# Scores for the softmax maxima spread over four row groups, in banks of three key tiles, interleaved with the scores of the weights

## The chip, the cores and the metric

The kernel runs on one core of a Trainium2 chip. The metric is device time in microseconds (us). The kernel before takes 2109.02 us, the median of three runs (2106.92 to 2109.55). One further execution was profiled; everything said of engines, waits and durations comes from its trace. TensorE (PE in the profile) multiplies matrices into PSUM, which has 8 banks of 128 x 512 float32; VectorE is DVE, ScalarE is ACT, GpSimd is POOL, SyncE is SP.

## The reference

Four blocks with residuals on x of shape (2, 1024, 512), all float32: a gated linear recurrence, a feed-forward block with ternary weights, differential attention, and the same feed-forward block again. The change touches the attention alone:

```
q = concat(heads(x @ Wq1), heads(x @ Wq2))       # 32 query heads, d = 32
k2, v2 = repeat(k, 2), repeat(v, 2)              # 16 heads of keys and values
scores = einsum('bhqd,bhkd->bhqk', q, k2) * scale
scores = where(causal, scores, finfo.min)
p = softmax(scores)
y = einsum('bhqk,bhkd->bhqd', p, v2)             # T = 1024 queries and keys
y = y1 - sigmoid(x @ Wlam) * y2
out = y @ Wo
```

A softmax needs the maximum of each query's row before the exponential. Queries and keys come in eight tiles of 128 each, so a head has 36 tiles of scores at or under the diagonal.

## The kernel before

The attention works on `pairs` of heads (L821): 32 pairs, in each of which the two heads are e = 0 and 1. Everything of a pair is made twice.

**Maxima.** The scores are first computed with queries on the partitions (`maxima_step`, L933; matmul L947, called s in the profile), and DVE reduces them along the keys to one negated maximum per query: `tensor_reduce` (L962) for blocks off the diagonal, and a masked form (L957) for blocks that end on it. Nothing but the maxima is kept. `split_maxima` (L967) writes each maximum as three bfloat16 parts on POOL, and `turn_maxima` (L983) transposes them on TensorE, so that they lie along the queries.

**Weights.** Then the scores are computed again with keys on the partitions (`weights_step`, L995; matmul L1008, called t), three rows of ones times the turned maxima are added in the same bank (L1016), ACT takes the exponential out of the bank (L1024), POOL zeroes what lies over the diagonal (L1027), and `weigh` (L1034; matmul L1046, called y) multiplies the weights with the values and accumulates in a bank of its own. A unit is one tile of 128 keys against one block of 512 queries or what of it the diagonal leaves (512, 384, 256 or 128 columns); there are 12 units, and a step takes two of them.

**Row groups.** A head has 32 dimensions, so a matmul of scores fills 32 of TensorE's 128 rows. Queries and keys are kept twice, in swapped halves, so that `operands(pair, i, e)` (L897) finds head e in row group 2i + e. Unit 0 of a step uses row groups 0 and 1, unit 1 uses 2 and 3. Each such float32 matmul becomes two weight loads and two matrix instructions in the profile.

**Order.** From the second part of the attention on, TensorE's instructions stand in the order of the source (`manual_schedule`, L1226); the loop is at L1228 to L1237. The other engines' order is made by a scheduler. A step of pair n is: the scores t of its two units (four banks), their subtractions, the maxima of three banks of pair n + 1, the products y of the step before, and then work `beside` it (projections, turned maxima, layer norms and so on). There are six steps to a pair, 31 pairs with a following one, and the maxima of pair 0 are made ahead of the loop between the products of `values`. The table `max_banks` (L920) spreads 18 banks of 512 columns over the six steps, three to a step, in three row groups.

**Banks.** Seven PSUM banks form one ring (`ps_ring`, L776; `ring_bank`, L780) for everything but y. A new tile takes the bank of the seventh tile before it, and its first matmul waits until that one's last reader is done.

Of the kernel before, what the change touches and what calls it, by code (L numbers as in the profile page):

```python
# [10 lines left out]
F32 = mybir.dt.float32  # L11
# [3 lines left out]
ALU = mybir.AluOpType  # L15
AX = mybir.AxisListType

P = 128
# [5 lines left out]
BLK = 512  # L24
# [18 lines left out]
def kernel(  # L43
# [15 lines left out]
    nc = tc.nc  # L59
# [66 lines left out]
    def layernorm_end(mv, rstd):  # L126
        nc.vector.reciprocal(rstd, rstd)
        return mv, rstd
# [103 lines left out]
    with ExitStack() as s:  # L232
# [65 lines left out]
        start = wa.tile([P, BLK], F32, name="a_start")  # L298
# [103 lines left out]
        first = Input(0)  # L402
# [27 lines left out]
        for t in range(NBLK):  # L430
            yt = wa.tile([P, NKC, BLK], F32, tag="yt", name=f"yt{t}")
            last = t == NBLK - 1
            for c in range(NKC):
                n = f"{t}_{c}"
# [9 lines left out]
                u = ap_.tile([P, BLK], F32, tag="u", name=f"u{n}")  # L444
                if t + c == 0:
# [3 lines left out]
                    following = Input(1, layernorm_end(*measured.root()))  # L449
# [22 lines left out]
                a = ap_.tile([P, BLK], F32, tag="a", name=f"a{n}")  # L472
# [53 lines left out]
                elif last and c == 1:  # L526

                    room = xt_pool.tile([P, NKC, D], F32, tag="xt", name="xn_f0_0")
# [9 lines left out]
            products = [(j, k) for j in range(TPB) for k in range(NKC)]  # L538
# [3 lines left out]
            po = {}  # L542
# [22 lines left out]
            if not last:  # L565
                q, rq = q_next, rq_next
                following = Input(t + 2, stats) if t + 2 < NBLK else None
# [11 lines left out]
    NQ = SEQ // P  # L579
# [188 lines left out]
    QB = BLK // P  # L768
    HV = HD + 1
    with ExitStack() as s:  # L770


        b_a, b_p, b_b, b_c, b_d = (
            s.enter_context(tc.tile_pool(name=f"b_{i}", bufs=1, reuse_waits="tile")) for i in "apbcd"
        )
# [4 lines left out]
        def ring_bank(name, dtype=F32):  # L780
            return ps_ring.tile(
                [P, BLK if dtype == F32 else 2 * BLK], dtype, tag="ring", name=name
            )


        causal = b_c.tile([P, BLK], BF, name="causal")
# [21 lines left out]
        for i in range(4):  # L808
# [12 lines left out]
        pairs = [  # L821
            (b, g, p, par)
            for b in range(NT // SEQ) for g in range(NG) for p in range(2) for par in range(2)
        ]
        groups, nmax, lams, totals, shares, factors = {}, {}, {}, {}, {}, {}
# [71 lines left out]
        def operands(pair, i, e):  # L897

            b, g, p, par = pair
            rows = ts(2 * i + e, HD)  # L900
            return (groups[b, g, kind][rows, int(i != p), :] for kind in (2, par))

        def name(pair):
            return "_".join(map(str, pair))
# [2 lines left out]


        fills = {
            "a": [(2, 0, 384), (0, 0, 128)],  # L910
            "b": [(1, 0, 256), (5, 512, 256)],
            "c": [(3, 0, 512)],
            "d": [(4, 0, 512)],
            "e": [(5, 0, 512)],
            "f": [(6, 512, 384), (4, 512, 128)],
            "g": [(6, 0, 512)],
            "h": [(7, 0, 512)],
            "i": [(7, 512, 512)],
        }
        max_banks = [  # L920
            [(e, i, fills[f]) for f, e, i in step]
            for step in (

                [("d", 0, 1), ("d", 1, 1), ("e", 0, 0)],
                [("c", 0, 1), ("a", 1, 1), ("a", 0, 0)],
                [("g", 0, 1), ("g", 1, 1), ("e", 1, 0)],
                [("c", 1, 1), ("b", 0, 1), ("b", 1, 0)],
                [("h", 0, 1), ("f", 1, 1), ("f", 0, 0)],
                [("h", 1, 1), ("i", 0, 1), ("i", 1, 0)],
            )  # L930
        ]

        def maxima_step(pair, step):  # L933


            if step == 0:
                nmax[pair] = b_a.tile(
                    [P, 2, NQ, 2], F32, tag="nmax", name=f"nmax{name(pair)}", bufs=2
                )
            maxima_of = nmax[pair].rearrange("p f j e -> p (f j e)")  # L940
            for x, (e, i, products) in enumerate(max_banks[step]):
                po = ring_bank(f"s{name(pair)}_{step}_{x}")
                keys, queries = operands(pair, i, e)
                at_col, made = 0, []
                for j, first, nk in products:
                    part = po[:, at_col : at_col + nk]
                    nc.tensor.matmul(  # L947
                        part, queries[:, ts(j, P)], keys[:, first : first + nk],
                        start=True, stop=True,
                    )  # L950
                    made.append((part, (first // BLK * NQ + j) * 2 + e, first + nk == (j + 1) * P))
                    at_col += nk
                for part, place, diagonal in made:
                    top = maxima_of[:, place : place + 1]
                    if diagonal:

                        nc.vector.tensor_tensor_reduce(  # L957
                            part, part, causal[:, BLK - part.shape[-1] :], -1.0, 3.0e38,
                            ALU.add, ALU.min, top,
                        )  # L960
                    else:
                        nc.vector.tensor_reduce(top, part, AX.X, ALU.max, negate=True)  # L962

        turned = {}
        n_maxima = [0]
# [1 line left out]
        def split_maxima(pair, half):  # L967

            m = maxima[n_maxima[0] % 4]
            n_maxima[0] += 1  # L970
            src = nmax[pair][:, 0, ts(half, QB), :]
            if half:
                nc.vector.tensor_tensor(src, src, nmax[pair][:, 1, ts(half, QB), :], ALU.min)
            part = m.rearrange("p j (d e r) -> p j d e r", d=2, e=2)
            rest = b_a.tile([P, QB, 2], F32, tag="mrest", name=f"mrest{name(pair)}_{half}", bufs=2)
            nc.gpsimd.tensor_copy(part[:, :, 0, :, 0], src)
            nc.gpsimd.tensor_sub(rest, src, part[:, :, 0, :, 0])
            nc.gpsimd.tensor_copy(part[:, :, 0, :, 1], rest)
            nc.gpsimd.tensor_sub(part[:, :, 0, :, 2], rest, part[:, :, 0, :, 1])
            nc.gpsimd.tensor_copy(part[:, :, 1, :, 0:3], part[:, :, 0, :, 0:3])  # L980
            turned[pair, half] = m
# [10 lines left out]
        units = [(qb, kb) for qb in range(2) for kb in range((qb + 1) * QB)]  # L992
        outs = {}

        def weights_step(pair, step):  # L995

            made, banks = [], {}
            for u in (2 * step, 2 * step + 1):  # L1000
                qb, kb = units[u]
                lo = max(0, kb - qb * QB) * P
                made.append((u, kb, lo, BLK - lo, kb >= qb * QB))
            for i, (u, kb, lo, nq, _) in enumerate(made):
                for e in range(2):
                    keys, queries = operands(pair, i, e)
                    banks[u, e] = ring_bank(f"t{name(pair)}_{u}_{e}")
                    nc.tensor.matmul(  # L1008
                        banks[u, e][:, :nq], keys[:, ts(kb, P)],
                        queries[:, (qb + 1) * BLK - nq : (qb + 1) * BLK],  # L1010
                        start=True, stop=False,
                    )
            for i, (u, kb, lo, nq, _) in enumerate(made):
                for e in range(2):
                    rows = slice(64 * i + 32 * e, 64 * i + 32 * e + 3)
                    nc.tensor.matmul(  # L1016
                        banks[u, e][:, :nq], ones[rows], turned[pair, qb][rows, lo:],
                        start=False, stop=True,
                    )
            steps = []  # L1020
            for u, kb, lo, nq, diagonal in made:
                pr = b_a.tile([P, 2, BLK], F32, tag="pr", name=f"pr{name(pair)}_{u}", bufs=4)
                for e in range(2):
                    nc.scalar.activation(pr[:, e, :nq], banks[u, e][:, :nq], AF.Exp)  # L1024
                if diagonal:

                    nc.gpsimd.affine_select(  # L1027
                        out=pr[:, :, :P], in_=pr[:, :, :P], compare_op=ALU.is_ge, fill=0.0,
                        base=0, pattern=[[0, 2], [1, P]], channel_multiplier=-1,
                    )  # L1030
                steps.append((pair, u, pr))
            return steps
# [115 lines left out]
        for n, pair in enumerate(pairs):  # L1148
            b, g, p, par = pair
            following = pairs[n + 1] if n + 1 < len(pairs) else None  # L1150
# [45 lines left out]
        n = len(pairs) - 1  # L1196
# [30 lines left out]
        waiting = []  # L1227
        for n, pair in enumerate(pairs):  # L1228
            for step in range(STEPS):
                made = weights_step(pair, step)  # L1230
                if n + 1 < len(pairs):
                    maxima_step(pairs[n + 1], step)
                for w in waiting:
                    weigh(*w)
                waiting = made
                for f, args in beside.get((n, step), ()):
                    f(*args)  # L1237
# [89 lines left out]
```

## Time and profile before

| | us |
|---|---|
| median of the runs | 2109.02 |
| the profiled execution | 2108.97 |
| its span, first to last instruction | 2107.3 |
| attention's loop over pairs and steps | 794.4 to 1705.0 of the span |
| TensorE's busy time in that loop | 909.48 of 910.60 |
| DVE's | 485.21 |
| ACT's | 379.51 |
| POOL's | 180.94 |

Times in the timeline are counted from the start of the span. A row such as "1106.30 1.03 PE L947 MATMUL s<-gr,gr 32*128 32x512 f32 x6" says: from 1106.30 on, for 1.03 us, TensorE ran six instructions of line 947, with 32 rows by 128 columns of weights, on 512 moving columns. Their ends are modelled. Brackets at the end of a row give the engine's idle time before it and who ended it. PEld is the loading of weights, which overlaps with matmuls.

### The profile page before, as it was taken

The page shows a single profiled execution, that of the slowest core. Times are in us where ns is not written, and L with a number is a line of the kernel's source. Part 1 is how long each engine was busy: PE and PEld are TensorE (multiplying, and loading weights), DVE is VectorE, ACT ScalarE, POOL GpSimd, SP SyncE. Part 2 cuts the span into 40 slices and gives each one's busy share as a digit, 9 for nine tenths or more (in the row PEclk, how much of TensorE's full clock was granted, in tenths as well). Part 3 has the DMA queues.
Part 4 walks back from the last instruction along what each step waited for, and adds up shares of the span by engine and source line. Part 5 has one row for each costly group of instructions (what it writes and reads, how often), then busy time and mean ns, then how long its engine had stood idle before and what let it go on. Part 6 is the DMA issues. An engine that isn't in the chain of part 4 may idle for free.

```text
span 2107.3 us, 28066 instructions
## 1 busy us (share of the span) xinstructions
PE 2087.2 (99%) x10624; PEld 1238.5 (59%) x10632; DVE 1102.9 (52%) x2279; ACT 826.1 (39%) x1581; POOL 461.5 (22%) x812
## 2 busy tenths in 40 slices
PE   8999999999999999999999999999999999999998
PEld 4444444788888844444444444444444447888887
DVE  5877778344345344545554555454546653443432
ACT  4444343333344313444344413244434523333432
POOL 1422313122121211212221213121212231122212
PEclk9999999999999999999999999999999999999999
DMA  7121212400000011111111101201010033000000
GB/s 274 60 90 60 90 75 77 193 1 1 1 1 14 22 47 48 37 29 36 31 37 24 41 8 38 60 17 48 20 33 14 14 113 135 20 1 21 1 21 20
DMA packets 50999, 98.71 MB, mean 47 GB/s; under 512 B 10800, under 2 KB 19120, under 8 KB 50864
## 3 DMA queue, kind: packets, MB, share of 16 engines
q1 hardware_dynamic: 50864, 96.93, 14.0%
q8 instruction: 83, 1.36, 0.3%
q14 instruction: 52, 0.43, 0.1%
HBM read 58.75 MB, written 16.78 MB: 36 GB/s over the span
## 4 chain that ended last, share of the span: by engine, by line
PE 94%; DVE 4%; issue 1%; POOL 0%; ACT 0%; DMA 0%; DVEq 0%; SPq 0%; ACTq 0%; POOLq 0%
PE y L1046 13%; PE g L664 11%; PE u L664 11%; PE f_out L685 11%; PE s L947 10%; PE pq L879 8%; PE t L1008 8%; PE pv L844 3%; PE pq L328 2%; PE a_out L546 2%; PE b_out L1115 2%; PE pa L328 2%; PE pv L328 2%; PE pg L328 2%; PE pk L328 2%; PE mt L987 1%
## 5 line engine op out<-in xcount | busy, mean ns | idle before, releaser
L1024 ACT ACTIVATE pr<-t 128x512 f32<-128x512 f32 (+3 forms) x768 | 314.8, 496 | 382.1 <-PE t L1016 381.9
L957 DVE CUSTOM_DVE_ANT_0 s<-s,causal 128x128 f32<-128x128 f32 (+3 forms) x512 | 245.2, 510 | 124.9 <-PE s L947 116.2
L1046 PE MATMUL y<-pr,val 128*64 128x512 f32 (+3 forms) x1536 | 292.0, 501 | 0.4 <-ACT ys L1063 0.2
L679 POOL TENSOR_TENSOR ssq<-ssq,sq 128x512 f32<-128x512 f32 x120 | 154.7, 1289 | 589.4 <-ACT sq L678 589.4
L962 DVE TENSOR_REDUCE nmax<-s 128x1 f32<-128x512 f32 x256 | 164.9, 686 | 182.7 <-PE s L947 182.6
L664 PE MATMUL g<-xs,w 128*128 128x512 f32 x1024 | 257.7, 394 | 0.0
L685 PE MATMUL f_out<-w,hs 128*128 128x512 f32 x1024 | 254.3, 390 | 0.3 <-DVE hs L673 0.3
L670 DVE TENSOR_TENSOR h<-h,u 128x512 f32<-128x512 f32 x128 | 88.0, 688 | 317.5 <-PE u L664 305.2
L664 PE MATMUL u<-xs,w 128*128 128x512 f32 x1024 | 253.2, 389 | 0.0
L947 PE MATMUL s<-gr,gr 32*128 32x512 f32 (+3 forms) x1536 | 251.0, 493 | 0.5 <-DVE nmax L957 0.5
L664 PEld LDWEIGHTS u<-xs,w 128*128 128x128 f32 x1024 | 192.2, 188 | 40.6
L685 PEld LDWEIGHTS f_out<-w,hs 128*128 128x128 f32 x1024 | 191.5, 188 | 40.6 <-DVE hs L673 1.1
L664 PEld LDWEIGHTS g<-xs,w 128*128 128x128 f32 x1024 | 190.0, 188 | 39.6 <-issue 1.0
L1046 PEld LDWEIGHTS y<-pr,val 128*64 128x64 f32 x1536 | 93.5, 136 | 180.8 <-issue 105.5
L1008 PE MATMUL t<-gr,gr 32*128 32x512 f32 (+3 forms) x1536 | 198.8, 533 | 0.0
L879 PE MATMUL pq<-b_xt,w_qk 128*128 128x512 f32 x384 | 176.0, 603 | 0.0
L947 PEld LDWEIGHTS s<-gr,gr 32*128 32x128 f32 x1536 | 148.5, 185 | 46.4 <-issue 14.6
L1027 POOL TENSOR_SCALAR_AFFINE_SELECT pr<-pr 128x256 f32<-128x256 f32 x256 | 102.1, 412 | 332.0 <-ACT pr L1024 332.0
L672 ACT CAST hs<-h 128x512 fp32r<-128x512 f32 x128 | 79.4, 620 | 234.3 <-DVE h L670 234.3
L669 ACT ACTIVATE h<-g 128x512 f32<-128x512 f32 x128 | 76.6, 599 | 230.6 <-PE g L664 230.5
L673 DVE TENSOR_TENSOR hs<-h,hs 128x512 fp32r<-128x512 f32 x128 | 88.6, 692 | 87.2 <-ACT hs L672 87.2
L879 PEld LDWEIGHTS pq<-b_xt,w_qk 128*128 128x128 f32 x384 | 69.7, 189 | 88.0 <-issue 74.0
(164 smaller groups left out, 2234.9 us busy)
## 6 DMA issues: line engine op xcount, KB each, us to landing
w<-w_kept SPq DMA_DIRECT2D x32, 768.0 KB, 8.6
w_kept<-w SPq DMA_DIRECT2D x16, 768.0 KB, 3.2
gr<-gr SPq DMA_DIRECT2D x96, 128.0 KB, 2.3
w<-in_w_gu_dram SPq DMA_DIRECT2D x32, 256.0 KB, 2.9
share<-ys SPq DMA_DIRECT2D x128, 64.0 KB, 2.0
x<-in_x_dram SPq DMA_DIRECT2D x16, 256.0 KB, 6.1
w<-in_w_pt_dram SPq DMA_DIRECT2D x16, 256.0 KB, 3.4
w_qk<-in_wq_dram SPq DMA_DIRECT2D x8, 512.0 KB, 4.2
```

Of the source, the lines that this page charges most:

```text
L328: nc.tensor.matmul(po, w[:, k, ts(c, P)], xt[:, k, :], start=(k == 0), stop=(k == NKC - 1))
L664: nc.tensor.matmul(po, ws[f][:, part, ts(k, P)], xs[:, e, k, :], start=(k == 0 and e == 0), stop=(k == NKC - 1 and e == 1),)
L679: nc.gpsimd.tensor_add(ssq, ssq, sq)
L685: nc.tensor.matmul(po[j], hp[:, e, ts(j, P)], ws[f][:, 2, :], start=(f == 0 and e == 0), stop=(f == NF - 1 and e == 1),)
L879: nc.tensor.matmul(po, w[:, k, ts(kind, P)], xts[b][:, k, ts(e, BLK)], start=(k == 0), stop=(k == NKC - 1),)
L947: nc.tensor.matmul(part, queries[:, ts(j, P)], keys[:, first : first + nk], start=True, stop=True,)
L957: nc.vector.tensor_tensor_reduce(part, part, causal[:, BLK - part.shape[-1] :], -1.0, 3.0e38, ALU.add, ALU.min, top,)
L962: nc.vector.tensor_reduce(top, part, AX.X, ALU.max, negate=True)
L1008: nc.tensor.matmul(banks[u, e][:, :nq], keys[:, ts(kb, P)], queries[:, (qb + 1) * BLK - nq : (qb + 1) * BLK], start=True, stop=False,)
L1024: nc.scalar.activation(pr[:, e, :nq], banks[u, e][:, :nq], AF.Exp)
L1027: nc.gpsimd.affine_select(out=pr[:, :, :P], in_=pr[:, :, :P], compare_op=ALU.is_ge, fill=0.0, base=0, pattern=[[0, 2], [1, P]], channel_mu ...
L1046: nc.tensor.matmul(y[64 * e : 64 * e + 64, lo:], all_values[:, HV * (NH * kb + h) : HV * (NH * kb + h) + 64], pr[:, e, : BLK - lo], start= ...
```

## The change

The maxima's 36 key tiles a head are cut anew: twelve pieces, most of three tiles (384 columns), some of two or four. 24 banks for the two heads take the place of 18; each step has four, one in each row group (`max_banks`). The reductions become 28 a pair in place of 24, and a query tile's maximum now comes from up to three pieces, so `split_maxima` has one more minimum for its second half.

`weights_step` becomes `row_phase`, and takes over the maxima of the following pair. Two banks for maxima (x = 0 and 1, row groups 2 and 3) are taken from the ring before all else. Then follow in TensorE's order: the scores of unit 0 (row groups 0 and 1), maxima 0 and 1 (row groups 2 and 3), the subtractions of unit 0, the scores of unit 1 (2 and 3), maxima 2 (0 or 1), the subtractions of unit 1, maxima 3 (the other of 0 and 1). The ring keeps its seven banks. Lines after the change are higher by up to 25: s is L949, t L1019, the subtraction L1029, y L1071.

```diff
         fills = {
-            "a": [(2, 0, 384), (0, 0, 128)],
-            "b": [(1, 0, 256), (5, 512, 256)],
-            "c": [(3, 0, 512)],
-            "d": [(4, 0, 512)],
...
+            "j01": [(1, 0, 2, 0), (0, 0, 1, 0)],
+            "j2": [(2, 0, 3, 0)],
+            "j3": [(3, 0, 4, 0)],
+            "j4a": [(4, 0, 3, 0)],
+            "j4b": [(4, 3, 2, 1)],
+            "j5a": [(5, 0, 3, 0)],
+            "j5b": [(5, 3, 3, 1)],
+            "j6a": [(6, 0, 3, 0)],
+            "j6b": [(6, 3, 3, 1)],
+            "j67": [(7, 7, 1, 2), (6, 6, 1, 2)],
+            "j7a": [(7, 0, 4, 0)],
+            "j7b": [(7, 4, 3, 1)],
         }
+
         max_banks = [
...
+            [(0, 1, "j2"), (1, 1, "j2"), (0, 0, "j5a"), (1, 0, "j4b")],
+            [(0, 1, "j3"), (1, 1, "j3"), (0, 0, "j01"), (1, 0, "j01")],
+            [(0, 1, "j5b"), (1, 1, "j5b"), (1, 0, "j5a"), (0, 0, "j4b")],
+            [(0, 1, "j4a"), (1, 1, "j4a"), (0, 0, "j6a"), (1, 0, "j67")],
+            [(0, 1, "j6b"), (1, 1, "j6a"), (1, 0, "j6b"), (0, 0, "j67")],
+            [(0, 1, "j7a"), (1, 1, "j7a"), (0, 0, "j7b"), (1, 0, "j7b")],
         ]
 
+        def maxima_bank(pair, step, x):
+            if step == 0 and x == 0:
+                nmax[pair] = b_a.tile(
+                    [P, 2 * NQ, 2], F32, tag="nmax", name=f"nmax{name(pair)}", bufs=2
+                )
+            return ring_bank(f"s{name(pair)}_{step}_{x}")
+
+        def maxima_of(pair, step, x, po):
+            tops = nmax[pair].rearrange("p j e -> p (j e)")
+            e, i, fill = max_banks[step][x]
+            keys, queries = operands(pair, i, e)
+            at_col, made = 0, []
+            for j, first, nk, slot in fills[fill]:
+                part = po[:, at_col : at_col + nk * P]
+                nc.tensor.matmul(
+                    part, queries[:, ts(j, P)], keys[:, first * P : (first + nk) * P],
+                    start=True, stop=True,
+                )
...
             if half:
-                nc.vector.tensor_tensor(src, src, nmax[pair][:, 1, ts(half, QB), :], ALU.min)
+                nc.vector.tensor_tensor(src, src, nmax[pair][:, NQ + QB : 2 * NQ, :], ALU.min)
+                top = nmax[pair][:, NQ - 2 : NQ, :]
+                nc.vector.tensor_tensor(top, top, nmax[pair][:, NQ + 2 : NQ + QB, :], ALU.min)
...
+            room = [maxima_bank(following, step, x) for x in range(2)] if following else []
+            scores(0)
+            for x, po in enumerate(room):
+                maxima_of(following, step, x, po)
+            subtract(0)
+            scores(1)
+            if following:
+                maxima_of(following, step, 2, maxima_bank(following, step, 2))
+            subtract(1)
+            if following:
+                maxima_of(following, step, 3, maxima_bank(following, step, 3))
...
             for step in range(STEPS):
-                made = weights_step(pair, step)
-                if n + 1 < len(pairs):
-                    maxima_step(pairs[n + 1], step)
+                made = row_phase(pair, pairs[n + 1] if n + 1 < len(pairs) else None, step)
                 for w in waiting:
                     weigh(*w)
```

In `max_banks` an entry is (head e, operand copy i, piece), and x is its place in the row; in `fills` it is (query tile, first key tile, number of key tiles, slot of the result).

## The prediction

> **What bounds the kernel now.** I read the page's busy times and its chain first, then the loop's stretch alone, then the timeline of single steps, last the groups of DVE.
>
> ```profile
> PE 2087.2 (99%) x10624; PEld 1238.5 (59%) x10632; DVE 1102.9 (52%) x2279; ACT 826.1 (39%) x1581; POOL 461.5 (22%) x812
> PE 94%; DVE 4%; issue 1%; POOL 0%; ACT 0%; DMA 0%; DVEq 0%; SPq 0%; ACTq 0%; POOLq 0%
> 794.40:1705.00 910.60, 909.48 (x6115) 433.69 (x6112) 485.21 (x1404) 379.51 (x885) 180.94 (x575) 1.00 0.12 31
> ```
>
> TensorE sets the end, and in the attention's loop it rests for 1.1 of 910.6 us. So a step's time is the time of TensorE's instructions in it, and whatever holds TensorE is paid in full. Two steps and a half of pair 10:
>
> ```profile
> 1101.60 0.70 PE L1008 MATMUL t<-gr,gr 32*128 32x256 f32 x8
> 1101.94 0.22 PE L1016 MATMUL t<-mt_s,ones 3*128 3x128 bf16 x2
> 1102.00 0.64 PE L947 MATMUL s<-gr,gr 32*128 32x512 f32 x2
> 1102.13 0.28 PE L1016 MATMUL t<-mt_s,ones 3*128 3x256 bf16 x2
> 1102.38 1.15 PE L947 MATMUL s<-gr,gr 32*128 32x384 f32 x8
> 1103.45 1.73 PE L1046 MATMUL y<-pr,val 128*64 128x512 f32 x8
> 1105.11 1.14 PE L1008 MATMUL t<-gr,gr 32*128 32x512 f32 x8
> 1106.07 0.40 PE L1016 MATMUL t<-mt_s,ones 3*128 3x512 bf16 x4
> 1106.30 1.03 PE L947 MATMUL s<-gr,gr 32*128 32x512 f32 x6
> 1106.55 2.07 ACT L1024 ACTIVATE pr<-t 128x512 f32<-128x512 f32 x4 [3.04 <-PE t L1016]
> 1107.26 0.87 PE L1046 MATMUL y<-pr,val 128*64 128x256 f32 x8
> 1107.36 1.89 DVE L962 TENSOR_REDUCE nmax<-s 128x1 f32<-128x512 f32 x3 [1.57 <-PE s L947]
> ```
>
> Let T be the start of a step's t. From T to y (the row phase) the full step takes 1107.26 - 1105.11 = 2.15 us: 0.107 for the first weight load, 0.853 for two passes of 512 columns, 0.227 for the subtractions, 0.853 for s, 0.10 to y. Four row groups run side by side, and they are independent: at 1101.94 the two short subtractions of unit 1, and at 1102.00 even s, start ahead of unit 0's subtractions (1102.13), which stand before them in the program.
>
> ```profile
> 889.67 0.41 PEld L1008 LDWEIGHTS t<-gr,gr 32*128 32x128 f32 x6 [0.17 <-issue]
> 890.27 0.18 PEld L1008 LDWEIGHTS t<-gr,gr 32*128 32x128 f32 x1 [0.20 <-ACT pr L1024]
> 890.27 0.13 PEld L1016 LDWEIGHTS <-ones 3*128 3x128 bf16 x3
> 892.40 0.20 PEld L1046 LDWEIGHTS y<-pr,val 128*64 128x64 f32 x4 [0.71 <-ACT pr L1024]
> ```
>
> This is what a wait costs. The fourth t of this step waited for its bank, which ACT still read, until 890.27; the subtractions behind it, of row groups that were free, started right after, not before. So a waiting instruction holds all behind it, whatever the row group. Row phase: 892.40 - 889.67 = 2.73 in place of the 2.26 of such a step without the wait (1109.08 to 1111.34).
>
> Worked out so over the 31 pairs with a following one, the six row phases last, on average, 2.144, 1.880, 2.149, 2.487, 2.137 and 1.638 (the fifth without two outliers of 3.13 and 6.56): 12.435 us a pair.
>
> **The change part by part.** *Streaming.* At 0.853 per 512 columns the after's row groups would be done thus. Steps 2 and 3 (both units 512): groups 0/1 carry t 0.853, subtraction 0.213, s 0.640; groups 2/3 s 0.640, t 0.853, subtraction 0.213; with lead-in 0.107 and 0.09 to y 1.90. Steps 0 and 4 the same, by groups 0/1. Steps 1 and 5 (units of 256 and 128): 1.37. Sum 10.35 a pair, 2.09 less than before. That would be -65 us over 31 pairs.
>
> *The bank.* Against this stands the ring. A step takes eight banks, in the order s0, s1, t, t, t, t, s2, s3, and the ring has seven; so s3 gets the bank of s0 of the same step, always, whatever lies beside. The changed program has it so: in every step the first matmul of s3 waits for DVE's reduction of s0. Before, s and t took seven, and no tile came back to its own step. When does s0 come free, from T?
>
> - TensorE's semaphore for s0. The trace's semaphore events of 1102.42 to 1102.52 come in program order, 0.034 apart, though unit 1's subtractions had ended at 1102.16; so I take s0's signal to wait for unit 0's t, which stands first and ends at 1.12 (1106.23 - 1105.11), plus 0.014: 1.134. In steps 1 and 5 s0 itself (512 columns) ends there.
> - DVE starts 0.023 later (median of the 181 reductions that waited).
> - From a reduction's start to its semaphore: masked 512 columns 0.769, 384 0.667; unmasked 512 0.694. Unmasked 384 does not occur before; 0.561 by the masked rows' 0.133 per 128.
> - Semaphore to weight load: 0.041.
>
> Then s3: weight load 0.107 (its group is idle by then), its columns, 0.089 to y.
>
> - Steps 0 and 2: s0 masked 384; s3 256 columns, 0.427: 1.134 + 0.023 + 0.667 + 0.041 + 0.107 + 0.427 + 0.089 = 2.49.
> - Steps 3 and 4: unmasked 384; s3 two products of 128, 0.436: 2.39.
> - Step 1: masked 512; s3 256 and 128, 0.645: 2.81.
> - Step 5: unmasked 512; s3 384, 0.640: 2.73.
>
> Sum 15.30, which is +2.87 a pair, +88.9 us over 31 pairs. Against before: +0.35, +0.93, +0.34, -0.09, +0.26, +1.09. Half of the loss is in the two short steps, where s0 and s3 are longer than the unit beside them.
>
> Behind s3's weight load stand the eight matmuls of y, then all that lies beside; they wait too, and need the whole array anyway. The 0.47 that half of the steps 3 lose to ACT is in the average above and goes: T comes later after the step before. Covered by that slack are ACT (four exponentials 2.07 us from T + 1.44, as before; unit 1's subtractions are signalled by 2.06, its turn on ACT comes at 2.47), POOL's masks behind them, and DVE: 28 reductions and one more minimum (0.167) a pair add some 0.8 us to about 13.7, in a pair of 28.9. With that cover gone each would hold the ring in the same way.
>
> *DVE late.* Where other work lies beside, s0's reduction comes behind it: 16 products with r (0.681 each) end four steps, eight additions of b_out (0.687) three more. About half of that work is left when s0 is signalled: 0 to 10 us, I take 4.
>
> *Start.* The maxima of pair 0 lie between products of values (six row phases of 1.07). Four of them lose 0.21 by the narrower banks: -1, between -1.3 and +1.
>
> Sum +92. The profiled execution (span 2107.3, 2108.97 in all) is 0.05 below the median, so 2109 + 92 = 2201.
>
> **A rule against the row.** The Trainium skill, "TensorE: Matmul & The Clock Gate", Part 3 on packing small matmuls, says that matmuls are strictly first in, first out, in start and in end. The rows at 1101.94 and 1102.13 contradict it for starts in different row groups. By the rule the new order would lose even without the ring: t of unit 1 could not start before unit 0's subtraction (T + 0.96), nor s3 before unit 1's (1.81), and a full step's row phase would be 2.33, +0.18; by the row it is 1.90. With the ring's wait s3 starts at 1.87 at the earliest, so the sum above holds by either.
>
> **The rivals.**
>
> 1. *Early signal.* If s0's semaphore is not held behind unit 0's t, it comes at s0's own end, 0.92, in steps 0, 2, 3 and 4: 0.21 earlier each, 26 us less: 2175. Without the 4 for DVE 2171. For it: t of unit 0 itself signals nothing. Against it: the order of signals seen.
> 2. *DVE is late in every step.* A reduction that meets DVE in another operation waits half of one, 0.3 us, in 186 steps: +56, 2257. For it: DVE is busy 53% of the loop. Against it: in a plain pair DVE has only these reductions, and the last of a step ends about 3.7 after T, while the next s0 is signalled no earlier than 3.36 + 1.13.
> 3. *The other side: the packing pays.* If s0's bank were free when s3's row group is (T + 1.17), the time would be 2109 - 65, 2044. It decides where the release in steps 0 and 2 comes before 1.48 and in 1 and 5 before 1.0 and 0.76. Against it: s0 of 512 columns streams until 0.96 in steps 1 and 5, before any reduction; masked 384 needs 0.75 to stream and 0.667 to reduce. Only a bank that is not shared would do it.
>
> **How the numbers follow.** The wait as worked out, 2201 within 15: 0.66. Early signal, about 2173: 0.14. DVE late, 2216 to 2257: 0.14. The packing pays: 0.05. No change, where both meet by accident: 0.01. The range reaches from the early signal less 5, 2166, to three quarters of the late-DVE case, 2245. Slower 0.94, faster 0.05, within 0.2% 0.01; 0.2%, some 4 us, is about what a measurement of this kernel can tell from no change.
>
> **What would show it.** In the changed profile: weight loads of s idle until DVE's nmax, some 0.5 us in each step and the longest in steps 1 and 5 (released by L960 or L965); row phases near 2.5, 2.8, 2.5, 2.4, 2.4 and 2.7; idle time of TensorE in the loop from 1 to some 30 us, in steps 1 and 5 (in the others unit 1's modelled ends, to 1.97, hide it); t's idle time behind ACT gone; everything outside the loop the same. I am wrong if s3 starts before DVE has read s0, if the row phases of steps 1 and 5 stay under 2, or if ACT or POOL is named where I name DVE.

## The result and the profile after

The changed kernel takes 2213.09 us, the median of four runs (2209.82 to 2213.14), against 2109.28 for the kernel before (2106.92 to 2109.92): 1.049 times as long, 95% interval 1.0472 to 1.0509. The forecast was 2201 with a range of 2166 to 2245: the sign, the mechanism and the range held, and the size was 12 us short.

From the changed kernel's profile page: the busy times, the chain that ended last, and the group of s's weight loads (busy time and mean of one, then the idle time ahead of them and who ended most of it).

```profile
PE 2159.1 (98%) x10888; PEld 1288.8 (58%) x10888; DVE 1113.1 (50%) x2439; ACT 831.4 (38%) x1581; POOL 460.5 (21%) x812
PE 91%; DVE 6%; issue 1%; POOL 0%; ACT 0%; DMA 0%; SPq 0%; DVEq 0%; ACTq 0%; POOLq 0%
L949 PEld LDWEIGHTS s<-gr,gr 32*128 32x128 f32 x1792 | 214.4, 184 | 125.7 <-DVE nmax L960 60.9
```

The stretch of the attention's loop in the changed kernel: start and end, length, then busy time (instructions) of PE, PEld, DVE, ACT and POOL, the granted clock, the DMA share and GB/s.

```profile
794.40:1809.00 1014.60, 981.31 (x6358) 484.00 (x6354) 494.51 (x1557) 385.01 (x885) 180.03 (x575) 1.00 0.11 28
```

The loop takes 1014.6 us where it took 910.6; all that lies outside it takes 1196.8 us where it took 1196.7. TensorE rests for 33.3 us of the loop where it rested for 1.1. The other 72 us (981.31 - 909.48) count as busy, though the columns are the same, 72 key tiles a pair: the modelled ends of matmuls reach into the wait (in step 2 of pair 10, below, unit 1's subtraction is counted until 1119.03, while s3 waits until 1118.95), and a page that says "98%" is compatible with a loop 11% longer. What shows the loss is who ends the idle time of s. The waits in the loop of the changed kernel (who waited, for whom: us in all, how many, the longest):

```profile
PEld s L949 <- DVE nmax L960: 60.1, 94, 1.0
PEld s L949 <- DVE nmax L965: 54.2, 93, 2.2
PE s L949 <- DVE nmax L960: 15.7, 34, 0.6
PE s L949 <- DVE nmax L965: 14.7, 32, 1.6
```

The first two rows count 187 waits, and there are 186 steps with a following pair: about one wait a step, a weight load of s that DVE's reduction releases. Before, the rows that answer to these were a few waits of s for DVE and 45 of t for ACT:

```profile
PEld t L1008 <- ACT pr L1024: 27.3, 45, 0.8
PEld s L947 <- DVE nmax L957: 7.5, 19, 1.3
```

The row of t behind ACT is gone from the changed kernel, as forecast. Steps 1 and 2 of pair 10 there, from the timeline of all engines:

```profile
1112.55 0.48 PE L1019 MATMUL t<-gr,gr 32*128 32x256 f32 x2
1113.72 0.70 DVE L960 CUSTOM_DVE_ANT_0 s<-s,causal 128x512 f32<-128x512 f32 x1 [0.50 <-PE s L949]
1114.53 0.72 PEld L949 LDWEIGHTS s<-gr,gr 32*128 32x128 f32 x4 [0.46 <-DVE nmax L960]
1115.38 1.72 PE L1071 MATMUL y<-pr,val 128*64 128x512 f32 x8
...
1117.03 0.70 PE L1019 MATMUL t<-gr,gr 32*128 32x512 f32 x2
1117.47 0.19 PEld L1019 LDWEIGHTS t<-gr,gr 32*128 32x128 f32 x2
1117.56 0.10 PEld L1029 LDWEIGHTS <-ones 3*128 3x128 bf16 x2
1117.99 0.38 PE L1029 MATMUL t<-mt_s,ones 3*128 3x512 bf16 x2
1118.27 0.57 DVE L960 CUSTOM_DVE_ANT_0 s<-s,causal 128x384 f32<-128x384 f32 x1 [1.60 <-PE t L1019]
1118.65 0.38 PE L1029 MATMUL t<-mt_s,ones 3*128 3x512 bf16 x2
1118.76 0.14 DVE L960 DVE_READ_ACCUMULATOR2_ANT nmax<- 128x1 f32 x1
1118.95 0.29 PEld L949 LDWEIGHTS s<-gr,gr 32*128 32x128 f32 x2 [0.55 <-DVE nmax L960]
1119.58 0.87 PE L1071 MATMUL y<-pr,val 128*64 128x256 f32 x8
```

In step 2 (T = 1117.03) DVE reduces s0 from 1118.27 and writes its result from 1118.76; at 1118.95, 0.05 us after that write's end, the weights of s3 are loaded, and at 1119.58 y follows. In step 1 the same chain (1113.72, 1114.53) makes a row phase of 2.83 us out of units that stream for little more than one. Taken over the 31 pairs, the row phases of the six steps (from the first weights of t to those of y), in us:

| step | before | forecast | after |
|---|---|---|---|
| 0 | 2.144 | 2.49 | 2.684 |
| 1 | 1.880 | 2.81 | 2.832 |
| 2 | 2.149 | 2.49 | 2.546 |
| 3 | 2.487 | 2.39 | 2.492 |
| 4, without two outliers | 2.137 | 2.39 | 2.493 |
| 5 | 1.638 | 2.73 | 2.766 |
| a pair | 12.435 | 15.30 | 15.81 |

(15.81 - 12.435) x 31 = 104.6 us, and the loop grew by 104.7 from its first t to its end. So the row phases hold the whole loss.

### The profile page after: what moved, and what is told of

Its sections match the earlier page's. It is cut to its first block, busy times and chain, and to the rows that moved or that the text cites. A ratio compares the mean times of both kernels' runs of the same rounds, so it can differ in the third digit from the quotient of the medians.

```text
span 2211.4 us, 28724 instructions
## 1 busy us (share of the span) xinstructions
PE 2159.1 (98%) x10888; PEld 1288.8 (58%) x10888; DVE 1113.1 (50%) x2439; ACT 831.4 (38%) x1581; POOL 460.5 (21%) x812
## 4 chain that ended last, share of the span: by engine, by line
PE 91%; DVE 6%; issue 1%; POOL 0%; ACT 0%; DMA 0%; SPq 0%; DVEq 0%; ACTq 0%; POOLq 0%
PE y L1071 12%; PE s L949 12%; PE g L664 11%; PE u L664 11%; PE f_out L685 10%; PE pq L879 8%; PE t L1019 7%; PE pv L844 3%; PE pq L328 2%; PE a_out L546 2%; PE b_out L1140 2%; PE pa L328 2%; PE pv L328 2%; PE pk L328 2%; PE pg L328 2%
## 5 line engine op out<-in xcount | busy, mean ns | idle before, releaser
L949 PE MATMUL s<-gr,gr 32*128 32x384 f32 (+3 forms) x1792 | 445.8, 472 | 32.5 <-DVE nmax L960 15.7
L960 DVE CUSTOM_DVE_ANT_0 s<-s,causal 128x128 f32<-128x128 f32 (+3 forms) x512 | 220.9, 457 | 150.7 <-PE t L1029 53.3
L1071 PE MATMUL y<-pr,val 128*64 128x512 f32 (+3 forms) x1536 | 292.0, 501 | 0.4 <-ACT ys L1088 0.3
L965 DVE TENSOR_REDUCE nmax<-s 128x1 f32<-128x384 f32 (+1 forms) x384 | 202.5, 573 | 176.5 <-PE t L1019 155.6
L949 PEld LDWEIGHTS s<-gr,gr 32*128 32x128 f32 x1792 | 214.4, 184 | 125.7 <-DVE nmax L960 60.9
L1019 PE MATMUL t<-gr,gr 32*128 32x512 f32 (+3 forms) x1536 | 283.1, 509 | 0.6 <-DVE nmax L965 0.6
L1019 PEld LDWEIGHTS t<-gr,gr 32*128 32x128 f32 x1536 | 129.1, 184 | 129.5 <-issue 76.7
L1071 PEld LDWEIGHTS y<-pr,val 128*64 128x64 f32 x1536 | 93.5, 136 | 136.0 <-issue 94.5
```

The lines of the kernel that those rows point to most:

```text
L949: nc.tensor.matmul(part, queries[:, ts(j, P)], keys[:, first * P : (first + nk) * P], start=True, stop=True,)
L960: nc.vector.tensor_tensor_reduce(part, part, causal[:, BLK - part.shape[-1] :], -1.0, 3.0e38, ALU.add, ALU.min, top,)
L1019: nc.tensor.matmul(banks[u, e][:, :nq], keys[:, ts(kb, P)], queries[:, (qb + 1) * BLK - nq : (qb + 1) * BLK], start=True, stop=False,)
L1071: nc.tensor.matmul(y[64 * e : 64 * e + 64, lo:], all_values[:, HV * (NH * kb + h) : HV * (NH * kb + h) + 64], pr[:, e, : BLK - lo], start= ...
```

## The experiments

All diffs are against the changed kernel.

The theory: s3 stands in the bank of s0 of the same step, so its first matmul waits until DVE has reduced s0, and everything behind it in TensorE's queue waits too. s0's signal comes in program order, behind unit 0's t. The rivals: the signal comes at s0's own end (early signal), DVE is late in every step, or the new mixed order itself costs (the rule of first in, first out across row groups), so that the fourth bank is not to blame.

**Three banks in the mixed order.** The old table of 18 banks, in the new order: s0 and s1 between the scores of the units, s2 after unit 1's. No bank comes back to its own step.

```diff
-            [(0, 1, "j2"), (1, 1, "j2"), (0, 0, "j5a"), (1, 0, "j4b")],
+            [(0, 1, "d"), (1, 1, "d"), (0, 0, "e")],
...
-            if following:
-                maxima_of(following, step, 3, maxima_bank(following, step, 3))
```

> The new order of a step with the old cut: three banks of 512 columns a step, the third maxima bank where the changed kernel has its third, and no fourth. A step then takes seven banks of the ring, and no tile comes back to its own step. If the shared bank is what the change costs, its loss is gone: row phases by the row groups' sums are 2.12 in the steps 0, 2, 3 and 4, 1.59 in step 1 and 1.58 in step 5, 11.7 us a pair against 12.4 before and 15.7 in the changed kernel, also because unit 1's scores come too late to meet the wait for ACT of steps 1 and 3. 2085 us, 2075 to 2097. Rival, the mixed order itself is dear (row groups with unlike work do not overlap freely): row phases stay near 2.5 and the time stays over 2150.

Measured: 2095.65 us (2094.72 to 2096.67) against 2107.62 for the kernel before in the same session, ratio 0.9942, interval 0.9928 to 0.9957. The order by itself costs nothing; it gains 12 us, and the result beats both kernels. The row phases are 2.130, 1.834, 2.148, 2.152, 2.137 and 1.638: five are what they were before or up to 0.05 less, and step 3 is 2.152 where it was 2.487, because no t waits for ACT any more (27.3 us of such waits before, none here). From this kernel's timeline, step 3 and the beginning of step 5 of pair 10:

```profile
1082.14 0.70 PE L1014 MATMUL t<-gr,gr 32*128 32x512 f32 x2
1083.10 0.38 PE L1024 MATMUL t<-mt_s,ones 3*128 3x512 bf16 x2
1084.29 1.94 PE L1064 MATMUL y<-pr,val 128*64 128x512 f32 x8
...
1090.49 0.48 PE L1014 MATMUL t<-gr,gr 32*128 32x256 f32 x2
1090.60 0.43 DVE L993 COPY mt_s<-mt 128x512 bf16<-128x512 bf16 x1 [0.67 <-PE mt L991]
1091.03 0.28 PE L1024 MATMUL t<-mt_s,ones 3*128 3x256 bf16 x2
1091.08 0.29 PEld L946 LDWEIGHTS s<-gr,gr 32*128 32x128 f32 x2
```

Step 3 goes from t to y in 2.15 us with nothing idle between. The gain is smaller than expected by some 10 us, in steps 1 and 5, expected at 1.59 and 1.58 and measured at 1.834 and 1.638. Both show at s2. In step 5 (the last four rows, T = 1090.49) its row group begins its last work, unit 0's subtraction, at 1091.03, but its weights load at 1091.08, which is 0.04 after DVE's signal at 1091.03 that the turned maxima are copied (1090.60). The trace has this delay of 0.04 from that signal in all 31 steps 5, and a semaphore to a weight load took 0.041 before. The turned maxima take a tile of the same ring just before this step, so s2 is the eighth tile from there on and most likely has their bank; that costs at most 0.05. In 29 of the 31 steps 1 s2's weights load at T + 0.775, at once after the last weights of s1's second product (T + 0.772), where those of step 5 load at T + 0.588. The 0.19 between them is nearly all of the 0.20 between the two row phases. What holds s2 there is open; its row group began its subtraction at T + 0.54.

**Four banks, s behind everything, as before the change.** The new table of 24 banks, in the old order: t, t, both subtractions, then s0 to s3.

```diff
             scores(0)
-            for x, po in enumerate(room):
-                maxima_of(following, step, x, po)
-            subtract(0)
             scores(1)
...
+            subtract(0)
             subtract(1)
             if following:
-                maxima_of(following, step, 3, maxima_bank(following, step, 3))
+                maxima_step(following, step)
```

> The new cut with the old order: all four scores of the weights, their subtractions, then the four maxima banks. Again eight banks a step; s3 now gets the bank of the first t of the same step, which ACT gives back at about T + 2.05 (512 columns: exponential starts at T + 1.44 and takes 0.60) or T + 1.28 in steps 1 and 5. If the eighth bank is the cause, the row phases are about 2.7, 2.2, 2.7, 2.7, 2.7, 2.2, and the time is near 2194 (2175 to 2215): slower than before in the old order too, with ACT named as the releaser of s instead of DVE. Rival, the mixed order is the cause: without it the narrower banks pay, 1.90 and 1.37, and the time is near 2044.

Measured: 2191.94 us (2189.49 to 2192.73), ratio 1.0397 (1.038 to 1.0415). The new table with its fourth bank, in the old order, costs 84 of the 104 us. The row phases are 2.71, 2.184, 2.71, 2.722, 2.722 and 2.176, against 2.7 and 2.2 expected. Here the bank that comes back to its own step is that of the first t, and ACT is the one waited for. The largest wait of s in this kernel's loop, in the form of the waits above:

```profile
PEld s L949 <- ACT pr L1044: 99.7, 153, 1.3
```

That is 153 waits behind ACT in 186 steps. Step 3 of pair 10 from the same kernel's timeline:

```profile
1113.25 1.14 PE L1019 MATMUL t<-gr,gr 32*128 32x512 f32 x8
1114.69 2.06 ACT L1044 ACTIVATE pr<-t 128x512 f32<-128x512 f32 x4 [0.69 <-PE t L1029]
1115.34 0.52 PEld L949 LDWEIGHTS s<-gr,gr 32*128 32x128 f32 x4 [0.69 <-ACT pr L1044]
1115.97 0.20 PEld L1066 LDWEIGHTS y<-pr,val 128*64 128x64 f32 x4
```

ACT begins its four exponentials at 1114.69; at 1115.34, when the first is signalled, s3's weights are loaded. So in both orders eight tiles a step on seven banks make a step wait for a reader of its own, and the order decides which reader it is.

**s0 reduced twice.** The changed kernel, with an unmasked reduction of s0's bank ahead of its own, meant to change nothing but s0's release, which comes later by that reduction.

```diff
+                if x == 0 and pair != pairs[0]:
+                    nc.vector.tensor_reduce(top, part, AX.X, ALU.max, negate=True)
```

> The changed kernel, with each piece of the first maxima bank (s0) reduced once more, unmasked, ahead of its own reduction; the result is the same. If s3 waits for s0's reduction in every step, each step grows by the spacing of one more reduction, 0.47 for 384 columns and 0.60 for 512: 3.1 us a pair, 95 over 31 pairs, 2213 + 95 = 2308 (2290 to 2325). DVE has the room for it: 3.1 in a pair of 32. Rival, TensorE's own work sets the step: 2213, unchanged within 10.

Measured: 2274.95 us in a single run, 62 over the changed kernel, where 95 were expected and 77 was the least. Against the changed kernel the row phases moved by +0.63, -0.24, +0.59, +0.59, +0.59 and -0.17: the four full steps pay the whole second reduction, and the two short ones, which should have paid most, became shorter. Two steps of pair 10 from this kernel's timeline, step 1 (T = 1130.52) and step 2 (T = 1134.76):

```profile
1131.69 0.69 DVE L959 TENSOR_REDUCE nmax<-s 128x1 f32<-128x512 f32 x1 [0.50 <-PE s L949]
1131.83 1.00 ACT L1051 ACTIVATE pr<-t 128x256 f32<-128x256 f32 x4 [0.56 <-PE s L949]
1132.26 0.72 PEld L949 LDWEIGHTS s<-gr,gr 32*128 32x128 f32 x4 [0.22 <-ACT pr L1051]
1132.53 0.70 DVE L962 CUSTOM_DVE_ANT_0 s<-s,causal 128x512 f32<-128x512 f32 x1
...
1136.01 0.56 DVE L959 TENSOR_REDUCE nmax<-s 128x1 f32<-128x384 f32 x1 [0.52 <-PE t L1021]
1136.60 0.57 DVE L962 CUSTOM_DVE_ANT_0 s<-s,causal 128x384 f32<-128x384 f32 x1
1137.27 0.29 PEld L949 LDWEIGHTS s<-gr,gr 32*128 32x128 f32 x2 [1.14 <-DVE nmax L962]
```

In step 2, s3 starts at 1137.27, behind both reductions: that is the theory. In step 1 it starts at 1132.26, released by ACT's first exponential, before the masked reduction of s0 has even begun (1132.53): s3 stands in a bank of t. In the built program this is so in 30 of the 31 steps 1 and in all 31 steps 5. In the steps 0, 2, 3 and 4 the trace has s3 released by DVE's second reduction in 123 of 124. So the wait for s0 is shown there, and the belief that a new tile always takes the bank of the seventh before it fell. In the changed kernel itself s3 has the bank of s0 in all 186 steps, but that is what the pool chose when it was built, not what it must choose. By what it chooses was not tried; that it goes by the bank that the scheduler expects to be free first would fit.

**Without s2.** The changed kernel without the products and reductions of s2, so that a step takes seven tiles and no bank comes back to its own step.

```diff
-            if following:
-                maxima_of(following, step, 2, maxima_bank(following, step, 2))
```

> The changed kernel without its third maxima bank, s2: its products and reductions are left out for all pairs but the first (the maxima of those pieces count as 0), the fourth bank s3 stays. Seven banks a step, so s3 no longer comes back to s0's bank. Of the row groups, the one that loses s2 was no longer than those of unit 1 in the full steps. If the shared bank is the cause, the row phases fall to the row groups' sums, near 1.90 in full steps and 1.37 in steps 1 and 5, from 15.7 to 10.4 a pair: about 2213 - 167 = 2046 (2035 to 2075). Rival, mixed order or the streaming of the remaining work sets the step: 2150 to 2205.

Measured: 2040.4 us in a single run. The row phases are 1.695, 1.500, 1.933, 2.014, 1.715 (without two outliers) and 1.424, in all 10.28 a pair, where 10.35 was worked out for row groups that only stream. The group of s's weight loads on this kernel's page:

```profile
L951 PEld LDWEIGHTS s<-gr,gr 32*128 32x128 f32 x1358 | 149.2, 184 | 12.8 <-DVE nmax L962 5.0
```

Their idle time is 12.8 us where it was 125.7. Step 2 of pair 10 (T = 1057.50) from its timeline:

```profile
1057.50 0.70 PE L1021 MATMUL t<-gr,gr 32*128 32x512 f32 x2
1058.46 0.38 PE L1031 MATMUL t<-mt_s,ones 3*128 3x512 bf16 x2
1058.68 0.37 PE L951 MATMUL s<-gr,gr 32*128 32x256 f32 x1
1059.12 0.38 PE L1031 MATMUL t<-mt_s,ones 3*128 3x512 bf16 x2
1059.43 0.76 PE L1071 MATMUL y<-pr,val 128*64 128x256 f32 x6
```

s3 starts at 1058.68, 1.18 after T, when its row group is done with the subtraction, and nothing of DVE stands between. The sum agrees better than its terms. In steps 2 and 3, where the scores of unit 1 and s0 or s1 set the end, 1.90 was worked out and 1.933 and 2.014 measured; in the short steps 1.37, and 1.500 and 1.424 measured; in steps 0 and 4 the 1.90 was that of s2's row group, which has nothing of s to do here, and s3's takes 1.695 and 1.715. With s2 in its place these two steps would be some 0.2 longer, 12 us in all, so I estimate about 2053 for the full work without a shared bank. That was not run: it needs an eighth bank, and y has it.

**s0 and s1 ahead of t.** The changed kernel, with s0 and s1 moved in front of unit 0's scores, so that their signals no longer stand behind those of t. Nothing else moves.

```diff
-            scores(0)
             for x, po in enumerate(room):
                 maxima_of(following, step, x, po)
+            scores(0)
             subtract(0)
```

> The changed kernel with the first two maxima banks ahead of unit 0's scores in TensorE's order, nothing else moved; s3 still gets s0's bank in every step. In the changed kernel's steps with 512 columns s0 ends 0.92 after T but its semaphore rises at 1.22, behind the two of unit 0's scores, which stand before it. If semaphores rise in the program's order and that holds s0, the new order frees it 0.30 earlier in steps 0, 2, 3 and 4, and s3 starts as much earlier: row phases near 2.4, 2.8, 2.25, 2.2, 2.2, 2.75; 1.2 us a pair, 37 less, 2176 (2165 to 2186). Rival, s0's semaphore rises with its own end, or DVE is the one that is late: 2213 within 5.

Measured: 2173.72 us (2172.77 to 2175.3), ratio 1.0306 (1.0289 to 1.0323) against 2109.02 in its session. That is 39 us less than the changed kernel, where 37 were expected if signals come in program order. Step 2 of pair 10 from its timeline (T = 1104.17):

```profile
1104.17 0.59 PE L949 MATMUL s<-gr,gr 32*128 32x384 f32 x2
1104.18 0.70 PE L1019 MATMUL t<-gr,gr 32*128 32x512 f32 x2
1105.11 0.57 DVE L960 CUSTOM_DVE_ANT_0 s<-s,causal 128x384 f32<-128x384 f32 x1 [1.30 <-PE s L949]
1105.79 0.29 PEld L949 LDWEIGHTS s<-gr,gr 32*128 32x128 f32 x2 [0.23 <-DVE nmax L960]
1106.42 0.44 PE L1071 MATMUL y<-pr,val 128*64 128x256 f32 x2
```

The same s0, with the same columns and the same row group, is reduced from T + 0.94 where it was T + 1.24, and s3 starts at T + 1.62 where it was T + 1.92. The row phases of the four full steps fell by 0.30 to 0.32 each, the short ones, where s0 itself ends as late as t's signals, by 0.03 to 0.04.

## Why the prediction was right, and where its sum was short

- *The fourth bank shares s0's, and its wait takes the gain and more.* Right, and shown three ways: the idle time of s is released by DVE once a step; with the release later by one reduction (s0 twice; 0.59 in step 2, from 1136.01 to 1136.60) the full steps are later by 0.59 to 0.63; without the sharing the row phases fall, to 12.04 a pair with all the work in three banks and to 10.28 without s2, which also takes work away. The reason given was too strong: "s3 gets the bank of s0 of the same step, always" holds in this program, but the program with s0 reduced twice has it otherwise in 61 of its steps 1 and 5.
- *Streaming, 10.35 a pair.* Right to within some 0.35: 10.28 without s2, and by estimate about 10.7 with 0.2 more in steps 0 and 4.
- *A waiting instruction holds all behind it.* The rows agree: in the two steps shown y starts 0.85 and 0.63 after s3's weights begin to load. They do not test it further than the prediction's rows at 890.27, since y needs all the rows of the array, s3's too.
- *"TensorE's semaphore for s0 ... 1.134".* The order was right (s0 ahead of t gains 39 us), the size was not, and this is the term of the sum that failed: 1.221 in the full steps. The working counted on unit 0's t signalling nothing. In the changed program they do signal: in step 0 of pair 10 (T = 1107.85) the trace has semaphore events of TensorE at 1108.984, 1109.027, 1109.069 and 1109.112, those of unit 0's two t first and then s0 and s1. The first stands at T + 1.136, where s0 was put; s0 comes two events later. 0.087 in four steps and 31 pairs are 10.8 us.
- *Step 0.* Forecast 2.49, measured 2.684; beside those 0.087, s0's reduction starts 0.14 later after T than in step 2 (1.383 against 1.244). It is the reduction that opens a new tile of maxima, and it carries two waits in the program, not one. 0.14 x 31 = 4.3 us. Which wait takes the time was not tried.
- *Reductions.* From start to signal the unmasked 384 columns, estimated at 0.561, take 0.569, and the masked 384, taken at 0.667, take 0.635. The masked 512 are as taken (0.768).
- *DVE late, +4.* Not seen: s0's reduction starts 0.023 after s0's signal in the median of steps 1 to 5, the outliers of step 4 add 5.4 us before and 5.4 after, and the steps' means hold little more than the terms above. The rival of a DVE that is late in every step (2257) falls with it.
- *Start, -1.* The first t comes 0.9 earlier.
- The sum: 15.8 us more in the row phases than worked out, 4 less for DVE, so 92 + 15.8 - 4 = 104, the measured loss. That the miss was 12 and not 16 is luck: a term that was not there covered a part of it.
- *The early signal (2175)* fell; its time was nearly reached by moving s0, not by leaving it. *The packing pays (2044)*: its condition, a bank that is not shared, gave 2040.4 without s2, by estimate some 2053 with it. Both prices were good within 10 us, the condition decided.
- *A rule against the row.* The Trainium skill, "TensorE: Matmul & The Clock Gate", Part 3, has matmuls first in, first out in start and end. By the prediction's working of the rule a full step without s2 would still last 2.33, since s3 there stands behind unit 1's subtraction; step 2 lasts 1.933. The rows without s2 show it: s3 starts at 1058.68, and unit 1's subtraction, which stands before it, at 1059.12. For the signals, on the other hand, program order is what the runs show.

## What to carry to other kernels

Count the tiles that one round takes from a ring of buffers: with one more tile than buffers the last must wait for a reader of its own round, and here all that stood behind it in TensorE's order paid for that wait. Where a result's reader is on the critical chain, put its producer first in program order, since its signal waits for those of what stands before it, even when those run on other row groups. And take the parts of a change apart: here the order was worth 12 us and the cut into four banks that came with it cost far more.

## What I had not expected of the hardware

- Signals of matmuls that end together come one by one, 0.043 us apart in the changed kernel's step 0. So a signal that nobody on the critical chain needs still delays those behind it.
- Neither weight loads nor matmuls of different row groups keep the order of the program. In step 2 of the changed kernel the weights of unit 1's t load at 1117.47 and those of unit 0's subtraction, which stands before it, at 1117.56; without s2, s3 starts 0.44 ahead of unit 1's subtraction (1058.68 and 1059.12).
